# Later due times for the two halves of a unit's output projection, in an attention and gated-delta-rule kernel on one core

## The chip, the core and the metric

The kernel runs on one core of a Trainium2 chip. A core has five engines that run side by side, each with an instruction queue of its own: TensorE for matrix products (PE in the profile, its weight loads PEld), VectorE (DVE), ScalarE (ACT), GpSimd (POOL) and SyncE (SP), which here only starts DMA transfers. They meet through semaphores. An engine works through its queue in order: when the instruction at its head waits, all behind it wait too. Matrix products are written to PSUM, a small memory of eight banks; everything else lies in SBUF or in DRAM. The metric is the device time of one execution in microseconds, and lower is better.

## What is computed

A transformer block on 16 sequences of 128 tokens, 256 wide, all in fp32: attention, then a gated delta rule layer ("the unit work" below), then a feed-forward part with per-sequence adapters and rounded weights. The change lies in the second of these. Cut to what matters:

```
mixed = silu(causal_conv(hidden @ W_qkv));  q, k, v = split(mixed)   # 16 key heads, 32 value heads, 128 each
z     = hidden @ W_z
core  = chunk_gated_delta_rule(q, k, v, g, beta)                     # chunks of 64 tokens
core  = core * rsqrt(mean(core * core, -1) + 1e-6) * norm_w
x     = x + (core * silu(z)) @ W_out
```

The output projection of the title is the last product, with `W_out`. The sum of squares of `core` over its 128 channels is needed before it, for the root.

## The kernel before

**Units.** The delta rule is cut into 64 units: one key head (with its two value heads) for a group of four sequences, 512 tokens. Units run group by group, 16 key heads each. The projections of one group's 16 units add up in two PSUM banks, one for each pair of sequences; so each unit's output projection has two halves, `project(0)` and `project(1)` in `finish_unit`. A half is four products of 128x128 weights (`z`) with 256 columns (`wo_head`), which appear as eight instructions on the chip. After the sixteenth unit of a group DVE adds the bank to `x_in`, and SP stores it.

**Slots and due times.** The work of a unit is spread over eleven slots. In every slot a new unit is started, so that ten or so units are worked on at once, each at another step. A slot has 24 parts. The table `TIMES` gives, for each step of a unit, its due time in parts since the unit began; the due time modulo 24 is its place in the slot, and the quotient says how many slots later it comes. A heap (`events`, drained by `run`) calls the steps in order of due time, and so writes the program in that order. Steps for DVE that follow a product are put into the same heap by `later`, some parts after it.

The places in a slot that matter here, in order. Each step belongs to another unit:

| place | step | engine work, line |
|---|---|---|
| 5 | second gate `gate(1)` | product `ps_z` L812 |
| 8 | `new_values(0)`, `(1)` | products `ps_y` L823, ACT copies them to `y` L824 |
| 9 | first value projection `val(0)` | product L467, ACT's first convolution tap L476 |
| 9.5 | **`project(0)`** | products `ps_out` L873 |
| 11 | `attend(0)` | products `ps_ot` L829, ACT squares into `sq` L833 |
| 12 | `lower` | 32x32 products `ps_lo` L737, ACT copies `Mi` L740 |
| 13 | second value projection `val(1)` | L467, L476 |
| 14 | `attend(1)` | L829, L833 |
| 15.5 | **`project(1)`** | L873 |
| 16.5 | `norms` | products of ones with the squared q and k, `ps_n` L509 |
| 16.5 | `root` | products of ones with `sq`, `ps_r` L842: the sum of squares |
| 19 | `grow` | 32x32 products `ps_up` L749 to L751 |
| 19 | logarithms: a table load on ACT (L547), then exp and ln | L549 to L556 |
| 20, 22.5 | `products` of keys and queries | `ps_kq` L586 |

**From root to projection.** `root` leaves the sum of squares in PSUM. DVE adds a constant term into `r`, ACT turns it into a reciprocal root by ln and exp (L552, L553), SP writes it to DRAM in four small transfers (`scales`, L850) and reads it back spread over all partitions (`rb`, L852), and at place 4 of the next slot POOL multiplies the unit's `z` by it (`norm`, L864). Then its two projection halves may run.

**What sets the order.** The framework lays out each engine's queue when the program is built. It follows the order in which the program was written, but issues a later instruction first where by its own reckoning the earlier one isn't ready. DVE's queue is kept in written order by hand (`InOrder`), and on ACT the functions of the two activation tables are tied together (`follow`). PE's queue has no such ties. Of PSUM, six banks (`ps_b`) rotate over all products except the output projection's, whose two banks are apart (`ps_r`).

**Buffers.** `z` and `wo_head` have two buffers each, `rb` and `y` one. `wo_head` for a unit is loaded by SP (L437), which waits in its queue until the second half of the unit before last has read the old contents.

**One slot in four.** Four units share an inverse of 32x32 blocks (`inverse`), whose first rows are short DVE instructions that fall into one slot of each four.

Of the kernel before, what the change touches and what calls it, by code (L numbers as in the profile page):

```python
# [58 lines left out]
def tile_adaln_attn_ffn(  # L59
# [852 lines left out]
    def residual(g, t):  # L912
# [14 lines left out]
        "last": [194.0],  # L927
        "values": [177.0, 181.0, 183.5, 191.0, 194.5, 195.5],
        "outputs": [217, 221, 224, 224, 227, 230, 232.5, 236],
        "finish": [244, 249.5, 255.5],  # L930
        "logs": [19.0],
    }
    lag_of = lambda name, i: int(TIMES[name][i] // BEAT)
# [312 lines left out]
```

## Time and profile before

The time is 2249.76 us, the median of three executions (2246.99 to 2257.99). The profile is of one more execution, which took 2258.01 us; its span, from the first to the last instruction, is 2256.3 us.

| | us or share | where it is read |
|---|---|---|
| profiled execution, its span | 2258.01, 2256.3 | times; head of the page |
| mean granted PE clock | 0.980 | list of cores |
| projection `ps_out`, 1024 matmuls | 251.7 busy, 390 ns each | costliest groups |
| POOL `norm` of `z`, 64 instructions | 151.2 busy, 2362 ns each | costliest groups |
| ACT's reason for waiting longest on PE in the delta rule, `cv` L476 for `ps_in` L467 | 76.3 | costliest groups |
| DMA queue of SP | 28.0% of 16 engines | DMA queues |
| PE busy in 356 to 1665 us | 1280.03 of 1309.00 | stretches |
| PE busy in 1665 to 1882 us | 184.81 of 217.00 | stretches |
| PE busy in 1882 to 2256 us | 363.74 of 374.00 | stretches |

How such a profile is read: the page gives busy times and their groups; the list of waits says which engine stood still before which instruction and what ended that; and the timeline gives start and length in order. The ends of matmuls are modelled, so two that follow each other closely overlap by some 0.1 us in the list; starts are the firmer numbers. In a timeline the columns are start in us, length in us, engine, line, operation, what is written and read, shape of the weights and of the moving data, and the number of instructions merged; a bracket at the end gives the idle time before it and what ended it.

### The profile page before, as it was taken

What the parts mean: (1) busy time and instruction counts of PE and PEld (TensorE: products, weight loads), DVE (VectorE), ACT (ScalarE), POOL (GpSimd) and SP (SyncE); (2) the same over time, 40 slices, a digit from 0 to 9 for tenths busy, and PEclk for the clock granted to TensorE, in tenths of its full rate; (3) what the DMA queues carried; (4) which work ended last, traced back from release to release, by engine and by line L of the source; (5) the groups of instructions that cost most, each with busy time, mean ns of one, the idle gap of its engine ahead of it and who ended that gap; (6) DMA issues with size and microseconds to landing.
All of it is one profiled execution on the core that took longest, in us unless ns stands there. A gap on an engine that the chain in (4) does not pass through costs nothing. (4 is left out here: it accounts for less than half of the span.)

```text
span 2256.3 us, 41245 instructions
## 1 busy us (share of the span) xinstructions
PE 2127.2 (94%) x15992; PEld 1297.5 (58%) x15992; DVE 1404.9 (62%) x2194; ACT 1365.7 (61%) x2373; POOL 831.6 (37%) x573
## 2 busy tenths in 40 slices
PE   7898689999999999999999999999998987999999
PEld 3444356666666666666666666666665663344445
DVE  4788887677686867768686777868665321311111
ACT  4778577777777777777777777777775661111110
POOL 2233535445262544526254452625444115400000
PEclk9999889999999999999999999999999998999999
DMA  2210123333334434333433433334333314000000
GB/s 60 70 44 25 55 64 88 96 103 100 96 107 113 112 93 107 98 97 107 114 111 93 107 99 96 106 101 115 93 103 94 99 56 153 0 5 17 10 5 14
DMA packets 303250, 182.14 MB, mean 81 GB/s; under 512 B 189393, under 2 KB 283345, under 8 KB 303057
## 3 DMA queue, kind: packets, MB, share of 16 engines
q1 hardware_dynamic: 300848, 175.00, 28.0%
q0 software_dynamic: 1344, 4.20, 0.6%
q8 instruction: 128, 2.10, 0.4%
q14 instruction: 66, 0.53, 0.1%
q10 hardware_dynamic: 864, 0.31, 0.1%
HBM read 152.69 MB, written 5.77 MB: 70 GB/s over the span
## 5 line engine op out<-in xcount | busy, mean ns | idle before, releaser
L79 DVE SCALAR_TENSOR_TENSOR cv<-ps_in,cw,cv 128x508 f32<-128x508 f32 (+2 forms) x768 | 567.1, 740 | 297.4 <-ACT cv L476 279.3
L873 PE MATMUL ps_out<-wo_head,z 128*128 128x256 f32 x1024 | 251.7, 390 | 35.7 <-POOL z L864 35.5
L864 POOL TENSOR_TENSOR z<-z,rb 128x1024 f32<-128x1024 f32 x64 | 151.2, 2362 | 310.9 <-DMA rb<-scales 264.7
L467 PE MATMUL ps_in<-hT,w_qk 128*128 128x512 f32 x512 | 249.0, 610 | 5.3 <-DVE cv L79 2.4
L467 PE MATMUL ps_in<-hT,w_v 128*128 128x512 f32 x512 | 248.6, 607 | 0.0
L873 PEld LDWEIGHTS ps_out<-wo_head,z 128*128 128x128 f32 x1024 | 190.7, 194 | 99.6 <-POOL z L864 67.8
L812 PE MATMUL ps_z<-hT,w_gate 128*128 128x512 f32 x512 | 241.9, 594 | 0.3 <-ACT M L776 0.3
L476 ACT ACTIVATE cv<-ps_in,cw 128x512 f32<-128x512 f32 x256 | 174.9, 683 | 77.9 <-PE ps_in L467 76.3
L638 POOL TENSOR_TENSOR prod<-lanes,inv 128x512 f32<-128x512 f32 (+1 forms) x64 | 129.5, 2045 | 121.3 <-DVE inv L79 121.3
L525 POOL TENSOR_TENSOR o<-off,lk 128x16 f32<-128x16 f32 x64 | 13.9, 217 | 414.8 <-ACT lk L555 414.8
L812 PEld LDWEIGHTS ps_z<-hT,w_gate 128*128 128x128 f32 x512 | 95.8, 190 | 114.4 <-issue 101.1
L829 PEld LDWEIGHTS ps_ot<-aT,y 128*128 128x128 f32 x1024 | 134.5, 192 | 38.1 <-issue 28.5
L586 PE MATMUL ps_kq<-kq 128*128 128x256 f32 x512 | 134.8, 407 | 15.4 <-DVE cv L79 14.0
L467 PEld LDWEIGHTS ps_in<-hT,w_qk 128*128 128x128 f32 x512 | 94.1, 195 | 85.9 <-issue 66.5
L823 PEld LDWEIGHTS ps_y<-v,W 128*128 128x128 f32 x1024 | 124.5, 192 | 30.6 <-issue 22.9
L570 ACT ACTIVATE kq<-cv 128x512 f32<-128x512 f32 x128 | 80.7, 630 | 97.8 <-DVE cv L79 97.6
L829 PE MATMUL ps_ot<-aT,y 128*128 128x128 f32 x1024 | 135.6, 275 | 1.7 <-ACT y L824 1.7
L638 POOL TENSOR_TENSOR prod<-inv,gm 128x512 f32<-128x512 f32 (+1 forms) x64 | 127.9, 2023 | 15.3 <-DVE gm L79 15.3
L823 PE MATMUL ps_y<-v,W 128*128 128x128 f32 x1024 | 124.8, 275 | 0.0
L467 PEld LDWEIGHTS ps_in<-hT,w_v 128*128 128x128 f32 x512 | 87.5, 190 | 64.1 <-issue 61.2
L529 POOL TENSOR_TENSOR aT<-aT,o 128x1024 f32<-128x1024 f32 x64 | 121.8, 1902 | 5.1
L586 PEld LDWEIGHTS ps_kq<-kq 128*128 128x128 f32 x512 | 94.7, 197 | 34.5 <-issue 9.4
(202 smaller groups left out, 4069.0 us busy)
## 6 DMA issues: line engine op xcount, KB each, us to landing
aT<-sums SPq DMA_DIRECT2D x64, 512.0 KB
rb<-scales SPq DMA_DIRECT2D x64, 512.0 KB
w_qk<-in_w_qkv_dram SPq DMA_DIRECT2D x128, 128.0 KB
w_v<-in_w_qkv_dram SPq DMA_DIRECT2D x64, 256.0 KB
w_gate<-in_w_z_dram SPq DMA_DIRECT2D x64, 256.0 KB
wo_head<-in_w_out_dram SPq DMA_DIRECT2D x64, 256.0 KB
diag<-bT SPq DMA_DIRECT2D x256, 32.0 KB
W<-Uc SPq DMA_DIRECT2D x256, 32.0 KB
```

What stands on the lines that cost most here:

```text
L79: ins = getattr(self.engine, name)(*args, **kw)
L467: T.matmul(ps, lhsT=w[:, c, blk, :], rhs=hTs[g][:, c, :], start=c == 0, stop=c == ND - 1)
L476: A.activation(cv, psv, AF.Copy, scale=cw[:, col, 3:4])
L529: G.tensor_tensor(t4, t4, o.rearrange("p s h i -> p (s h) i")[:, :, :, None].to_broadcast([P, NP, 2, C]), ALU.subtract)
L570: ins = A.activation(dst, src, AF.Silu)
L586: T.matmul(ps[:, j, :, :], lhsT=d["kq"][:, s, 0, :], rhs=d["kq"][:, s, :, :], start=True, stop=True)
L638: G.tensor_tensor(out_tile, lhs[:, :, None, :].to_broadcast([P, r, c, j]), rhs.rearrange("p j c -> p c j")[:, None, :, :].to_broadcast([P, ...
L812: T.matmul(ps, lhsT=w_gate[u][:, c, h * P : (h + 1) * P], rhs=hTs[g][:, c, :], start=c == 0, stop=c == ND - 1)
L823: T.matmul(ps[:, j, :], lhsT=d["W"][:, p, :], rhs=v[:, p, :], start=True, stop=True)
L829: T.matmul(ps[:, s * S : (s + 1) * S], lhsT=d["y"][:, 2 * s + h, :], rhs=d["aT"][:, 2 * s + h, :], start=True, stop=True)
L864: G.tensor_tensor(d["z"], d["z"], d["rb"], ALU.mult)
L873: T.matmul(ps[:, j, :], lhsT=d["z"][:, h, s * S : (s + 1) * S], rhs=w_o[u][:, h, :], start=kh == j == h == 0, stop=kh == NK - 1 and j == h ...
```

## The change

Two due times are moved: the first half from 249.5 to 251.5, the second from 255.5 to 258.0. In places of a slot that is 9.5 to 11.5 and 15.5 to 18. POOL's `norm`, at 244, keeps its time. Nothing is computed differently, no buffer changes, and the slot in which each step falls stays the same (`lag_of("finish", ...)` and `LAST` are 10 before and after).

```diff
         "outputs": [217, 221, 224, 224, 227, 230, 232.5, 236],
-        "finish": [244, 249.5, 255.5],
+        "finish": [244, 251.5, 258.0],
```

In the order of due times, `project(0)` goes from behind `val(0)` to behind `attend(0)`, ahead of `lower`; `project(1)` goes from behind `attend(1)` to behind `norms` and `root`, ahead of `grow`. For the last unit of a group, the DVE addition into `x_in` and the store that follow a half move with it.

## The prediction

> **What bounds the kernel now.** I read the page's busy table first, then the costliest groups.
>
> ```profile
> PE 2127.2 (94%) x15992; PEld 1297.5 (58%) x15992; DVE 1404.9 (62%) x2194; ACT 1365.7 (61%) x2373; POOL 831.6 (37%) x573
> ...
> L873 PE MATMUL ps_out<-wo_head,z 128*128 128x256 f32 x1024 | 251.7, 390 | 35.7 <-POOL z L864 35.5
> ```
>
> TensorE (PE) is the bound, and the moved matmuls (L873, "the projection") are the group before which it idles longest. The busy time by stretch splits the run: 0 to 356 us attention and filling, 356 to 1665 the steady slots (PE busy 1280 of 1309 us), 1665 to 1882 draining, then the FFN. The change acts in the second and third. PE's waits inside the second:
>
> ```profile
> PE ps_kq L586 <- DVE cv L79: 14.0, 13, 1.6
> PE ps_out L873 <- POOL z L864: 11.2, 21, 1.1
> ```
>
> So two thirds of the 35.5 us lie outside the steady slots (10.6 of them before the last unit's projection alone). With PE 98% busy there, whatever PE gains or loses in a steady slot moves the end. One slot in PE's order of time (start, length, line):
>
> ```profile
> 997.73 1.99 PE L873 MATMUL ps_out<-wo_head,z 128*128 128x256 f32 x8
> 999.56 1.05 PE L829 MATMUL ps_ot<-aT,y 128*128 128x128 f32 x8
> 1000.54 0.69 PE L737 MATMUL ps_lo<-Tc,bT 32*32 32x32 f32 x32
> 1001.17 1.98 PE L467 MATMUL ps_in<-hT,w_v 128*128 128x512 f32 x4
> 1002.99 1.05 PE L829 MATMUL ps_ot<-aT,y 128*128 128x128 f32 x8
> 1003.88 1.89 PE L873 MATMUL ps_out<-wo_head,z 128*128 128x256 f32 x8
> 1005.70 0.64 PE L509 MATMUL ps_n<-sqa,ones 128*32 128x256 f32 x8
> 1006.16 0.61 PE L842 MATMUL ps_r<-sq,ones 128*32 128x256 f32 x8
> ```
>
> This is the source order of the due times: first half (9.5), attend 0 (11), lower (12), second value projection (13), attend 1 (14), second half (15.5), norms and root (16.5). The new times put the first half behind attend 0 and the second behind norms and root.
>
> **What the first half gains.** A unit's z is ready a nearly fixed time after its second value projection, and PE waits for it in the slots where DVE was late. Without a wait the half starts 0.43 us after the last value matmul. Over units 0 to 54 I summed what each start lies above that: 16.2 us. A half that waited also runs 1.99 instead of 1.89 us, 3.2 us in all. (The waits table says less because it counts from modelled ends, which overlap 0.16 us.) Behind attend 0 the half is due 0.89 us later (1003.88 less 1002.99); all but 1.0 us of the excess is smaller than that, and the later second part takes the rest. **Gain 19.4 us.** Attend 0 now needs y directly after the value projection. The copy of y ends 0.5 to 0.9 us early in half of the slots, 0.0 in a quarter, 0.2 us late in the last quarter; since the slot before it will be longer by what follows, I take 1 us of 0 to 3.
>
> **What the second half covered.** Root reads sq, which ACT squares from attend 1's bank. ACT in that slot:
>
> ```profile
> 1002.07 0.63 ACT L570 ACTIVATE cv<-cv 128x512 f32<-128x512 f32 x1
> 1002.72 1.28 ACT L547 ACT_TABLE_LOAD   x1
> 1004.01 0.69 ACT L476 ACTIVATE cv<-ps_in,cw 128x512 f32<-128x512 f32 x1
> 1004.60 0.59 ACT L833 ACTIVATE sq<-ps_ot 128x512 f32<-128x512 f32 x1
> ```
>
> Square waits behind the convolution's first tap and that behind a table load, and ends at 1005.19; root at 1006.16 is 0.97 us late for it only because the half lies between. With the half gone, norms follow attend 1 at once. Slot 9 has no projection yet (the first unit's comes in slot 10) and shows exactly this order:
>
> ```profile
> 333.58 1.05 PE L829 MATMUL ps_ot<-aT,y 128*128 128x128 f32 x8
> 334.57 0.64 PE L509 MATMUL ps_n<-sqa,ones 128*32 128x256 f32 x8
> 335.51 0.64 PE L842 MATMUL ps_r<-sq,ones 128*32 128x256 f32 x8 [0.31 <-ACT sq L833]
> ```
>
> There attend 1 to norms is 0.99 us, and root starts 0.05 us after square's end (335.46), leaving PE idle. In the steady slot: norms at 1002.99 + 0.99 = 1003.98, root could start 0.46 later (1006.16 less 1005.70), at 1004.44, and must wait until 1005.19 + 0.05 = 1005.24. **Stall 0.80 us.** Square ends 1.15 us after attend 1 in 41 of units 1 to 54. In the other 13, every fourth, the table load comes later, square ends at 1028.48 against an attend 1 begun at 1026.79, and the stall is 0.29 us; but there PE already idles 0.67 to 1.6 us a little later, before ps_kq, for a bank that DVE frees on its own time, so it is swallowed. Cost 41 x 0.80 = 32.8 us.
>
> Here two rules of the Trainium skill change the sum. "TensorEngine Tiling (Array Packing)", Key Properties, says tiles of one mode run in parallel but switching the mode drains TensorE. Parallel: the page's group rows give 398 ns for a norms matmul, and eight in series would cover 3.2 us and leave no stall; the timeline's 0.46 us shows the column strips beside each other. Drain: before, 128x128 goes to 128x32 to 32x32; now it goes to 128x32, back to 128x128 and to 32x32, one switch more per unit. The row for a switch is 0.99 less 0.89: 0.1 us, 93 ns in the finer steps, so 41 x 0.093 = 3.8 us (the 13 others again swallow it). "ScalarE: Activation LUTs", What ACT_TABLE_LOAD costs, puts a switch of tables at about 1.28 us plus a 1.38 us drain. By it square would end 1.38 us later, the stall would be 2.18 us and the sum 89 us (about 2323); in the trace the load takes 1.28 and the next activation starts 0.01 us after it, so 0.80 stands.
>
> **Does root's earlier place help z?** No: DVE makes r only after the second value convolution's taps (1004.73 to 1007.03), the norms' two operations and attend's product, at 1008.01; root had ended at 1006.77. **Queues passed.** SP holds wo_head's load until the second half has read the old weights: issued at 1005.80 before, about 1007.7 now; the next SP issue is at 1009.35, behind r, and an issue takes 0.37 us, so 1.3 us are spare. POOL's norm stays. The halves use two PSUM banks of their own, so the rotation of six keeps its order; norms and root wait only on ACT, whose copies of Mi end at 1002.05. DVE's eight sums into x_in come behind r instead of before it, at most a gain. Behind root on PE stand the second half, grow and ps_kq: all 0.9 us later, which is the cost above.
>
> **Drain.** There z is late by up to 3.8 us, and the half stands already where the compiler's planner thought z ready, so its due time matters little. Without norms, square is unfinished right after attend 1 and the second half goes first, as now. Where the planner let a projection break into a root, the rest of root now precedes the second half: I take -2 us of -5 to +2.
>
> Sum: 32.8 + 3.8 + 1 - 19.4 - 2 = +16.2 us on the profiled execution's 2258.0. That run lies 8.3 us above the median shown; added to the median 2249.8 it gives **2266.0 us**.
>
> **Rivals.** The order on an engine is the planner's: it keeps source order but takes a later instruction where it thinks the earlier not ready. On ACT the table load (due 19) runs ahead of a tap due 13 and a square due 14.
>
> *The half slips between norms and root* (14%), if the planner's own estimate has square unfinished after norms. Then root starts no earlier than now: no stall, but two extra switches, 41 x 0.2 = 8.2 us; 8.2 + 1.0 (excess left) + 3 (y) - 19.4 - 2 = -9.2: 2240.6, not slower. It decides from the point where norms are reckoned shorter than square's delay. For it: the real numbers, 0.46 against 1.15. Against it: slot 9, where grow was next and root still came first, with PE idling; and the drain:
>
> ```profile
> 1733.74 1.05 PE L829 MATMUL ps_ot<-aT,y 128*128 128x128 f32 x8
> 1737.16 0.91 PE L842 MATMUL ps_r<-sq,ones 128*32 128x256 f32 x2 [2.36 <-ACT sq L833]
> 1741.89 6.52 PE L873 MATMUL ps_out<-wo_head,z 128*128 128x256 f32 x16 [3.82 <-POOL z L864]
> 1748.34 0.63 PE L842 MATMUL ps_r<-sq,ones 128*32 128x256 f32 x6
> ```
>
> The projection entered after one quarter of a root, and again at 1844.38; two hits on a gap of 7 ns would be strange, so the planner seems to reckon the quarters in series, and norms as long enough.
>
> *Square moves up* (10%): attend 0 and its square come earlier, ACT is freer, and the table load falls behind the square, as it does in every fourth slot. Stall 0.29 us: 41 x 0.29 + 3.8 + 1 - 19.4 - 2 = -4.7, 2245. Against it: the load takes the hole while the second value projection still runs, and that hole stays.
>
> *The stall without the gain* (6%): z becomes later with PE (a later bank or load), and the wait stays: 32.8 + 3.8 = +36.6, 2286.
>
> **Numbers.** The stall has 70%; its own range is 2256 to 2280 (stall 0.6 to 1.0 us, gain 14 to 20). 0.5% is 11.2 us, about what a measurement tells from no change. Above 2261: 0.54 of the 0.70, and the last rival, 0.60. Below 2238.5: half of the first two rivals, 0.12. Between: 0.28. The range 2240 to 2284 leaves out half of the first rival, some of the last and the tails.
>
> **What would show it.** Right: root preceded by some 0.8 us idle for ACT sq in three of four slots, projection waits for POOL z nearly gone from the steady slots, ps_kq waits smaller, steady slots about 0.3 us longer on average. Wrong: the second half between norms and root, or square before the table load.

## The result, and the profile after

The changed kernel takes 2263.03 us (median of 15 executions, 2258.88 to 2268.5); the kernel before takes 2253.85 us in the same comparison (15 executions, 2246.99 to 2257.99). The ratio is 1.0044, interval 1.0035 to 1.0054: slower by 9.2 us where 16.2 were forecast. The profiled execution of the changed kernel took 2261.17 us, span 2259.5.

First the page's busy table and the row of the projection:

```profile
PE 2143.2 (95%) x15992; PEld 1281.6 (57%) x15992; DVE 1403.0 (62%) x2194; ACT 1362.1 (60%) x2373; POOL 832.6 (37%) x573
...
L873 PE MATMUL ps_out<-wo_head,z 128*128 128x256 f32 x1024 | 271.5, 399 | 28.7 <-POOL z L864 28.5
```

PE is busy 16 us longer with the same 15992 instructions, and the projection alone accounts for all of it: 271.5 us instead of 251.7, as the profile of before has it (the row stands in the prediction). So the products did not only wait elsewhere, they also ran longer. PE's list of waits in the steady slots (356 to 1665 us; us in total, times, longest):

```profile
PE ps_r L842 <- ACT sq L833: 4.2, 10, 0.6
PE ps_vt L795 <- DVE aT L79: 3.3, 3, 1.4
PE ps_kq L586 <- ACT W L753: 3.0, 3, 1.2
PE ps_kq L586 <- DVE cv L79: 2.2, 4, 1.4
PE ps_out L873 <- POOL z L864: 0.9, 3, 0.4
```

The projection's wait for z has gone (11.2 to 0.9 us), and the ps_kq wait for DVE has shrunk from 14.0 to 2.2 us (3.0 us before ps_kq now stand against ACT). But the stall that was to carry the loss, ps_r for ACT's sq, is 4.2 us in 10 slots and not 32.8 in 41. One slot in PE's timeline shows why:

```profile
1002.24 1.05 PE L829 MATMUL ps_ot<-aT,y 128*128 128x128 f32 x8
1003.23 0.64 PE L509 MATMUL ps_n<-sqa,ones 128*32 128x256 f32 x8
1003.80 0.70 PE L873 MATMUL ps_out<-wo_head,z 128*128 128x256 f32 x2
1004.50 0.64 PE L842 MATMUL ps_r<-sq,ones 128*32 128x256 f32 x8
1005.06 1.56 PE L873 MATMUL ps_out<-wo_head,z 128*128 128x256 f32 x6
```

The framework slipped one of the half's four products (two instructions) in between norms and root, and left three behind root. So it is in 50 of the 53 steady slots; in the other three (17, 33 and 49, the first slot of a group) two products slipped in. That is neither the order of the forecast (the whole half behind root) nor that of the first rival (the whole half between). It fills PE until the square is ready. ACT's timeline of the slot:

```profile
1001.97 1.28 ACT L547 ACT_TABLE_LOAD   x1
1003.27 0.69 ACT L476 ACTIVATE cv<-ps_in,cw 128x512 f32<-128x512 f32 x1
1003.85 0.59 ACT L833 ACTIVATE sq<-ps_ot 128x512 f32<-128x512 f32 x1
```

Square ends at 1004.44, as late behind attend 1 (2.20 us after its start) as before; root starts 0.06 us later, at 1004.50. ACT's order is as it was; what changed is PE's.

**Where the time went.** I cut each of the 53 steady slots (those of the projections of units 1 to 53, counted from one) at the starts of five PE groups and added up. Starts are used because the ends are modelled.

| stretch, us over 53 slots | before | after | difference |
|---|---|---|---|
| `val(0)` to `lower` (holds the first half) | 253.4 | 238.3 | -15.1 |
| `lower` to attend 1 | 129.5 | 129.5 | 0 |
| attend 1 to `grow` (holds the second half) | 196.9 | 232.0 | +35.1 |
| `grow` to `ps_kq` | 48.9 | 39.7 | -9.2 |
| `ps_kq` to the next `val(0)` | 679.8 | 674.1 | -5.7 |
| sum | 1308.5 | 1313.6 | +5.1 |

The two profiles differ by 3.2 us only, since the one of before has two stretches at lower clock that the other lacks: a mean granted clock of 0.83 in 330 to 350 us and 0.79 in 437 to 445, against 1.00 in the corresponding stretches of after. The profile of before starts its steady slots 3.4 us later, and its fourth slot takes 1.4 us longer (14.37 us from `ps_kq` where after has 12.95). If both are put down to the lower clock, the difference without them is 3.2 + 3.4 + 1.4 = 8.0 us, near the 9.2 of the medians.

### The profile page after: what moved, and what is told of

Read it like the earlier page. It is cut to its first block, busy times and chain, and to the rows that moved or that the text cites. A ratio compares the mean times of both kernels' runs of the same rounds, so it can differ in the third digit from the quotient of the medians.

```text
span 2259.5 us, 41250 instructions
## 1 busy us (share of the span) xinstructions
PE 2143.2 (95%) x15992; PEld 1281.6 (57%) x15992; DVE 1403.0 (62%) x2194; ACT 1362.1 (60%) x2373; POOL 832.6 (37%) x573
## 5 line engine op out<-in xcount | busy, mean ns | idle before, releaser
L873 PE MATMUL ps_out<-wo_head,z 128*128 128x256 f32 x1024 | 271.5, 399 | 28.7 <-POOL z L864 28.5
L467 PE MATMUL ps_in<-hT,w_v 128*128 128x512 f32 x512 | 248.2, 607 | 0.0
L873 PEld LDWEIGHTS ps_out<-wo_head,z 128*128 128x128 f32 x1024 | 182.9, 193 | 100.6 <-issue 48.6
L638 POOL TENSOR_TENSOR prod<-lanes,inv 128x512 f32<-128x512 f32 (+1 forms) x64 | 129.5, 2047 | 119.1 <-DVE inv L79 119.1
L1153 POOL TENSOR_TENSOR o<-o,x_in 128x512 f32<-128x512 f32 x8 | 10.1, 1265 | 279.3 <-DVE o L79 279.3
```

The lines of the kernel that those rows point to most:

```text
L467: T.matmul(ps, lhsT=w[:, c, blk, :], rhs=hTs[g][:, c, :], start=c == 0, stop=c == ND - 1)
L638: G.tensor_tensor(out_tile, lhs[:, :, None, :].to_broadcast([P, r, c, j]), rhs.rearrange("p j c -> p c j")[:, None, :, :].to_broadcast([P, ...
L873: T.matmul(ps[:, j, :], lhsT=d["z"][:, h, s * S : (s + 1) * S], rhs=w_o[u][:, h, :], start=kh == j == h == 0, stop=kh == NK - 1 and j == h ...
```

## The experiments

All runs compute the whole result. The kernel before took 2256.88 us beside e1 to e4 and 2256.42 beside the others. The stretches are summed as above; "rest" is `lower` to attend 1 and `ps_kq` to the next `val(0)`.

| kernel | us | ratio, interval | first half | second half | `grow` to `ps_kq` | rest | sum |
|---|---|---|---|---|---|---|---|
| before | | | 253.4 | 196.9 | 48.9 | 809.3 | 1308.5 |
| after | 2263.03 | 1.0044, 1.0035 to 1.0054 | 238.3 | 232.0 | 39.7 | 803.6 | 1313.6 |
| e1 | 2254.17 | 0.9993, 0.9980 to 1.0006 | 237.3 | 197.0 | 53.0 | 827.1 | 1314.5 |
| e2 | 2271.37 | 1.0064, 1.0042 to 1.0085 | 258.1 | 226.5 | 38.0 | 801.1 | 1323.8 |
| e3 | 2274.62 | 1.0088, 1.0066 to 1.0111 | 249.8 | 214.5 | 41.4 | 828.2 | 1333.9 |
| e4 | 2282.78 | 1.0119, 1.0098 to 1.0140 | 238.0 | 250.3 | 40.3 | 805.2 | 1333.9 |
| e5 | 2238.62 | 0.9918, 0.9903 to 0.9932 | 237.2 | 196.9 | 51.2 | 809.6 | 1294.9 |
| e6 | 2241.84 | 0.9925, 0.9910 to 0.9939 | 239.6 | 196.9 | 53.4 | 808.9 | 1298.7 |
| e7 | 2257.05 | 1.0002, 0.9991 to 1.0012 | 239.0 | 225.8 | 40.3 | 805.1 | 1310.1 |
| e9 | 2261.23 | 1.0015, 1.0004 to 1.0027 | 248.2 | 214.5 | 41.6 | 811.9 | 1316.2 |

And the second half's stretch in its three steps, mean us of the slots of the third place in each four (there the first half hardly waited, so little mixes in):

| kernel | attend 1 to norms | norms to root | root to `grow` | order |
|---|---|---|---|---|
| before | 2.71 | 0.46 | 0.54 | half, norms, root |
| after | 0.98 | 1.27 | 2.06 | norms, 1 product, root, 3 products |
| e2 | 0.98 | 1.63 | 1.63 | norms, 2 products, root, 2 products |
| e3, e9 | 0.98 | 2.49 | 0.57 | norms, half, root |
| e4 | 0.98 | 1.26 | 2.49 | norms, root, half |
| e7 | 0.98 | 0.76 | 2.49 | norms, root, half; square early |

**e1: the first half alone.** It asks whether the gain is there without the loss.

```diff
-        "finish": [244, 249.5, 255.5],
+        "finish": [244, 251.5, 255.5],
```

> Only the first half is moved (251.5), the second stays at 255.5. Both theories of the loss put it into the second half, so they agree here: attend 1 to grow stays 3.71 us in every slot, and the first half's lateness in the steady slots (18.6 us over 53 slots before) falls to about 2: 2253.9 - 16.5 = 2237 us. A rival says that the wait for z only hides DVE's lateness and is passed on to ps_kq or to y: then 2250 us and the waits before ps_kq (14.0 us) or ps_ot grow by what ps_out loses.

The steady gain came, 16.1 us in the first half's stretch, and yet the time didn't move. The three slots in which a group ends (16, 32, 48) grew from 78.5 us to 95.1 together, and that took back as much. One of them, DVE's timeline:

```profile
732.57 0.68 DVE L79 TENSOR_TENSOR x_in<-ps_out,x_in 128x512 f32<-128x512 f32 x1
...
739.78 0.69 DVE L79 TENSOR_TENSOR x_in<-ps_out,x_in 128x512 f32<-128x512 f32 x1 [3.66 <-DMA x_in<-in_x_dram]
...
741.74 0.25 DVE L79 TENSOR_SCALAR nn<-ps_n 128x128 f32<-128x128 f32 x1
```

SP's queue in the same stretch:

```profile
733.28 0.37 SPq L879 DMA_DIRECT2D x<-x_in  x1
733.74 0.42 SPq L437 DMA_DIRECT2D wo_head<-in_w_out_dram  x1
736.98 0.37 SPq L447 DMA_DIRECT2D x_in<-in_x_dram  x1
```

And PE, behind it:

```profile
736.50 2.98 PE L586 MATMUL ps_kq<-kq 128*128 128x256 f32 x8 [1.66 <-ACT W L753]
742.05 3.78 PE L467 MATMUL ps_in<-hT,w_qk 128*128 128x512 f32 x4 [2.57 <-DVE nn L79]
```

`x_in` has one buffer. After the first half DVE adds into it, SP stores it, and only then can SP load the other pair's `x_in`, which DVE needs after the second half. Sum to sum takes 7.2 us here; the halves now lie four parts of a slot apart instead of six, and DVE, in written order, stands 3.66 us with `nn` behind the wait. PE needs the bank that `nn` frees. Then the clock falls: `ps_in` takes 3.78 us where it takes 1.88 in an ordinary slot, and the mean granted clock in 735 to 750 us is 0.66.

**e2: the second half alone.**

```diff
-        "finish": [244, 249.5, 255.5],
+        "finish": [244, 249.5, 258.0],
```

> Only the second half is moved (258.0). The order laid out has two of its four products between norms and root in 41 slots. If the two moves add up (total +9.2, first half alone -16.5), this costs +25.7: 2279 us. If instead the slot's lengthening by 0.6 us alone already takes most of the wait for z away, whichever half causes it, the first half's gain is spent only once: +35 in attend 1 to grow, -9 before ps_kq, -14 of the wait for z: 2262 to 2266 us.

14.5 us slower, between the two forecasts. The waits for z stay, PE's list in the steady slots:

```profile
PE ps_out L873 <- POOL z L864: 14.3, 20, 1.9
```

So the second half's move does nothing for z and costs; the first half's move is what removes the wait. Root's stall is 1.0 us here, because in 40 of the 53 slots two products were slipped in before root instead of one. In the other 13, the fourth of each four, where square ends earlier, it was one.

**e3: the whole half between norms and root.** In these and the next runs two explanations of the 35 us stand against each other: that each stay of the half's 128x128 products inside the narrow run of norms, root and `grow` has a price of its own (about 0.3 us ahead of root and 0.2 behind it), or that only the prediction's 0.1 us for a switch and the stall count.

```diff
-        "keys": [0, 5.0, 9.5, 9.0, 15.0, 16.5, 32.5],
+        "keys": [0, 5.0, 9.5, 9.0, 15.0, 16.4, 32.5],
...
-        "finish": [244, 249.5, 255.5],
+        "finish": [244, 251.5, 256.45],
```

> The whole second half stands between norms and root (due 256.45, norms 16.4), the first at 251.5. Root comes when square has long ended, so there is no stall. Theory W (a stay of 128x128 products among the 128x32 ones costs 0.2 to 0.3 us beyond its own matmuls): attend 1 to grow 4.02 us in every slot, against 3.71, 2250 us. Theory S (the wait for square is the loss, a switch costs 0.09): 3.92 us in every slot, 2246 us.

From attend 1 to `grow` it takes 4.05 us in every slot, against 3.71 before: 0.34 more with no stall at all (root starts 0.73 us or more after square's end). The total was missed by 24 us. The halves are again too close at a group's end: its three slots take 93.8 us, 15.3 more than before, and the three behind them (17, 33, 49) 83.1 instead of 75.0. e9 repeats it without that.

**e4: the half held behind root.** A tie makes the forecast order come true:

```diff
-                T.matmul(ps[b], lhsT=ones, rhs=d["sq"][:, :, :, b], start=True, stop=True)
+                table["root"] = T.matmul(ps[b], lhsT=ones, rhs=d["sq"][:, :, :, b], start=True, stop=True)
...
+                    if n == 1 and j == h == 0:
+                        follow(ins, table["root"])
```

with the due times of the change.

> The first half at 251.5, the second at 258.0 and tied behind root's last product, so nothing can slip between norms and root: the order that the prediction had. Root then waits for square with PE idle, 0.80 us in three of four slots. As predicted (a switch 0.09): attend 1 to grow 4.60 us there, 2270 us. With theory W on top: 4.73 us, 2277 us. If the stall does not come, 3.9 us and 2246 us.

The predicted stall is there as soon as the predicted order is. PE's timeline of one slot, and the entry of its list of waits:

```profile
1013.96 0.64 PE L509 MATMUL ps_n<-sqa,ones 128*32 128x256 f32 x8
1015.22 0.64 PE L842 MATMUL ps_r<-sq,ones 128*32 128x256 f32 x8 [0.62 <-ACT sq L833]
1015.79 1.99 PE L873 MATMUL ps_out<-wo_head,z 128*128 128x256 f32 x8
```

```profile
PE ps_r L842 <- ACT sq L833: 29.8, 42, 1.2
```

Norms to root is 1.26 us instead of 0.46, so the stall is 0.80 us, as the prediction had it, and the list (which counts it from modelled ends) has it in 42 slots. In the first place of each four it is 1.11 us, in the fourth 0.40. The kernel is 25.9 us slower than before, more than the prediction's 16.2: from attend 1 to `grow` it takes 4.74, that is 3.71 + 0.80 + 0.23, not 3.71 + 0.80 + 0.09.

**e5 and e6: the first half alone, without the collision at a group's end.** e5 keeps the old times for the sixteenth key head; e6 moves all first halves and gives `x_in` two buffers, both loaded ahead.

```diff
-        "finish": [244, 249.5, 255.5],
+        "finish": [244, 251.5, 255.5],
...
-                plan(n - lag, make(at(lag)), TIMES[name])
+                edge_unit = name == "finish" and at(lag)[0] == NK - 1
+                plan(n - lag, make(at(lag)), [244, 249.5, 255.5] if edge_unit else TIMES[name])
```

```diff
-            if g == NG - 1:
-                load_x(g, 1)
+            load_x(g, 1)
...
-        kw = dict(tag="M2", bufs=2) if g == NG - 1 and n else dict(tag="x_in")
+        kw = dict(tag="M2", bufs=2) if g == NG - 1 and n else dict(tag=f"x_in{n}")
...
-                if n == 0 and g < NG - 1:
-                    load_x(g, 1)
```

> The first half at 251.5 for 60 units, and at its old 249.5 for the four that end a group. Theory X: the first half's gain is real, and moving it alone gave it back in the three slots where a group ends, because DVE's sum of the second half then waits for the second x_in, whose load can't start before the first half's sum is stored from the same buffer. Then the three slots fall from 95.1 us in all to the 78.5 of before, the rest keeps its gain of 10 to 14 us, and the time is about 13 us under the kernel before. If the gain was only passed on to DVE (the rival), it stays within 4 us of before.

> The first half at 251.5 for all units, but x_in has a buffer for each half and both are loaded before the group ends. Theory X: DVE does not wait for x_in, the three slots take 76 to 79 us, and the time is about 13 us under before, as with the four units left at their old time. If it is something else that moving the first half does at the end of a group (the bank, the store), the three slots stay near 95 us.

Both come out: 17.8 and 14.6 us faster than before, with 78.6 and 79.3 us for the three group ends. PE's list of waits in e5 no longer has z, and keeps the ps_kq wait, since nothing was added that could use it up:

```profile
PE ps_kq L586 <- DVE cv L79: 14.9, 17, 1.6
PE ps_in L467 <- DVE aT L79: 4.1, 16, 0.3
```

e5 and e6 can't be told apart (2236.53 to 2242.09 us, 2236.43 to 2243.34), and both beat the kernels before and after.

The two moves don't add up. e5's -17.8 and e2's +14.5 would make after 3 us faster than before, and it is 9 us slower. Of these 12.5 us, 5.5 lie in the second half's stretch (232.0 in after, 226.5 in e2, where two products instead of one fill the wait for the square). Where the rest lies was not shown.

**e7: as e4, with the table load held behind the square.**

```diff
         for ins in table["silus"]:
             follow(block[0], ins)
+        if "square" in table:
+            follow(block[0], table["square"])
...
-            A.activation(d["sq"][:, h].rearrange("p s t -> p (s t)"), ps, AF.Square)
+            table["square"] = A.activation(d["sq"][:, h].rearrange("p s t -> p (s t)"), ps, AF.Square)
```

> As the run with the second half forced behind root, and on ACT the table load is tied behind attend 1's square. If the table load is what makes square late, it ends 0.64 us after attend 1 in every slot instead of 1.15, the stall before root falls from 0.80 to 0.29 us, and attend 1 to grow takes 4.2 to 4.35 us in all slots instead of 4.74 (5.04): 41 x 0.5 = 20 us less than that run, 2262 us. If something else holds square, 4.74 us stays.

25.7 us faster than e4. ACT's timeline of one slot, and PE's:

```profile
1002.64 0.60 ACT L835 ACTIVATE sq<-ps_ot 128x512 f32<-128x512 f32 x1 [0.20 <-PE ps_ot L831]
1003.26 1.28 ACT L547 ACT_TABLE_LOAD   x1
```

```profile
1002.54 0.64 PE L509 MATMUL ps_n<-sqa,ones 128*32 128x256 f32 x8
1003.29 0.64 PE L844 MATMUL ps_r<-sq,ones 128*32 128x256 f32 x8
```

Norms to root is 0.76, a stall of 0.30 us where e4 has 0.80: the other half microsecond was the table load's place ahead of the square. It only brings the forecast order back to the level of before, though: its second half's stretch is still 28.9 us longer than before, by the stay of the half behind root and what is left of the stall, and the first half's gain (14.4) and the shorter waits behind `grow` (12.8) only just make up for it.

**e9: e6 with the whole half between norms and root**, the norms and second half at the due times of e3.

> The whole second half between norms and root again, now with two x_in buffers. Theories W and X together: attend 1 to grow stays 4.05 us, the slots at a group's end lose nothing, and the 20 to 25 us above the expectation of 2250 us vanish: 2248 to 2254 us, about the kernel before. If the half between norms and root costs more than its 0.34 us per slot in some other place, 2265 us or more stays.

The group ends are repaired (79.4 us instead of e3's 93.8), and attend 1 to `grow` is 4.05 again. The total is 7 us above the upper end of what was expected. Part of it can be placed, in PE's list of waits (lines are one lower here):

```profile
PE ps_out L872 <- POOL z L863: 7.9, 6, 1.9
```

The first unit's z in a group comes 20.1 to 22.1 us after the end of its root instead of 17.9, and ACT's ln and exp of `r` take 2 to 3.5 us together where they take 0.87 elsewhere: in slot 17 a convolution tap stands between them. Why ACT's order differs there stays open.

## Why the prediction was right or wrong

The direction and the range were right, in part by luck. Two terms of the sum were wrong and made up for each other in part: the stall was 26 us too high and the switch of mode 18 us too low. Of the prediction's own signs, the waits for z and ps_kq shrank as it said, but root's idle 0.8 us in three of four slots did not come, and the sign of being wrong, the second half between norms and root, came in part.

- **What the first half gains**: right in kind and nearly in size. 15.1 us in after, 16.1 and 16.2 in e1 and e5 where it stands alone, against 19.4 less 1 for y. The list has no wait of attend 0 for y in the steady slots. What is left of it lies in the first slot of each four (4.67 us from `val(0)` to `lower` against 4.43 in the others), where DVE is nearly full (below).
- **What the second half covered**: the stall of 0.80 us was the right price of the wrong order. e4 shows it to the hundredth when the half is held behind root. In after the framework issued one product between norms and root, and the stall fell to 0.06 us in two slots of four, about 0.35 in the first (14 slots), none in the fourth. Together that is 6.5 us (what the 35.1 leave beyond the 28.6 of the next point) instead of 32.8. The step that failed is the argument from slot 9 and the drain that the framework "seems to reckon ... norms as long enough" for the square: those places showed what it does when the next step is `grow` or when a root is already under way, not when four ready products stand behind root. e2, where fewer slip in when the square ends earlier, fits a reckoning that takes the square for unready after norms. But how it reckons readiness is not visible in a trace, and no run here settles it.
- **The switch of mode, 0.093 us per unit**: mis-sized. "TensorEngine Tiling (Array Packing)", Key Properties, in the Trainium skill says that a switch drains TensorE, and I priced it by the one switch that the trace of before shows. A stay of wide products inside the narrow run costs more. With 0.216 us for each of the half's instructions in a row (1.82 less 0.09 from half to norms in before, divided by eight), what is left over between norms and root is 1.21 - 0.46 - 2 x 0.216 = 0.32 us in after's slots without stall, 1.63 - 0.46 - 4 x 0.216 = 0.31 in e2, and 2.49 - 0.46 - 8 x 0.216 = 0.30 in e3. Between root and `grow` it is 2.06 - 0.54 - 6 x 0.216 = 0.22 in after, 0.23 in e2, 0.22 in e4. The price hangs on the place and not on the number of products. Two stays are 0.54 us per slot, 28.6 us in 53; the one switch ahead of norms only changes its place (0.98 less 0.89 before, now at attend 1). The weight loads (PEld) show where a part of the price arises. The first line is before, the second after:

```profile
1003.77 1.60 PEld L873 LDWEIGHTS ps_out<-wo_head,z 128*128 128x128 f32 x8
1003.79 0.30 PEld L873 LDWEIGHTS ps_out<-wo_head,z 128*128 128x128 f32 x2 [0.41 <-issue]
```

  In all 53 slots of before the half's first load starts 0.11 us ahead of its first product (1003.88), under attend 1's products, and root's first load 0.21 us ahead of root, under the norms. In after both start with their product (1003.80 for the half), so neither load is hidden. 0.11 + 0.21 is as much as a stay ahead of root costs. For the stay behind root this explains 0.11 of the 0.22; the rest is open, and no run tests it.
- **Swallowed by the ps_kq wait**: right, and more than reckoned. The fourth slots lose 0.55 us at the second half and get 0.71 back before ps_kq.
- **In some slots another engine is nearly full**: missed. The mean slot by its place in the four (without slots 4, 16, 32 and 48, which the lower clock and the group ends lengthen):

| place | before | after | e5 |
|---|---|---|---|
| first | 24.96 | 24.93 | 24.62 |
| second | 24.30 | 24.42 | 23.81 |
| third | 23.87 | 24.41 | 23.82 |
| fourth | 25.17 | 24.88 | 25.13 |

  In the first place after's stretches trade against each other: unit 17 has 5.07 us in the first half's and 4.24 in the second half's stretch, unit 53 has 4.43 and 4.86, and both slots last 24.95 to 24.98. The second half's stretch is 0.89 us longer there on average, but 0.34 comes back behind ps_kq (12.93 to 12.59) and 0.57 in the first half's stretch. So nearly the full 0.60 us is paid in the third place alone; in the second, the first half's 0.48 covers most of it. The prediction's 41 x 0.893 assumed it in three places of four. In slot 25 of after, a first one, DVE is busy 23.41 of 24.93 us and PE 24.40; in the two slots behind it DVE is busy 14.50 and 13.40 us and PE all of 24.4. So DVE probably holds the first place. It is not shown: with e4's longer stall the first place grew to 25.35 us, so PE counts there too.
- **Queues passed**: the statement that DVE's later sums into `x_in` are "at most a gain" holds for after only because both halves moved (sums some 6.5 parts apart; DVE waits 2.5 us for x_in in two groups). e1 shows the same step as a loss of 16.6 us. On SP one item was missed: at a group's end the second half's store now goes ahead of the root's four transfers.

```profile
739.29 0.37 SPq L879 DMA_DIRECT2D x<-x_in  x1
739.75 2.68 SPq L850 DMA_DIRECT2D scales<-r  x4
```

  `r` was ready at 738.07, so `scales` waits 1.7 us, and z comes 19.84 us after root's end instead of 17.91. It falls into slots of the first place (17, 33, 49), which last 24.65 to 24.98 us like their like, so no cost is seen.
- **Drain**: -2 was taken, and the part behind the last steady slot is 1.4 us longer in after (594.8 against 593.4 us), 1.3 longer in e2 and 4.9 shorter in e5 (588.5). By these single profiles, with stretches at lower clock in the drain (a mean of 0.95 over 1665 to 1882 us in after), the first half's move helps there and the second half's does not; the prediction treated them together.
- **Rivals**: "the half slips between norms and root" was half true, one product of four. Its price of two switches at 0.2 us together should be 0.34 by e3, and for after's split 0.54. At e3's price over 53 slots (18.0 us instead of 8.2) its -9.2 becomes +0.6, and e9, which has that order without the group-end loss, is at 1.0015. "Square moves up" is what e7 builds: its stall of 0.29 us was right (0.30), its total of 2245 was not (2257.05), mostly for the same missing price of the stay.

Sum over the steady slots: first half -15.1, stays +28.6, stalls +6.5, given back in the last two stretches of the table -14.9 (of it 1.4 the lower clock in the profile of before), in all +5.1.

Set beside the forecast: 16.2, less 26.3 for the stall, plus 17.8 for the stays (21.6 us in the 40 slots outside the fourth place, instead of 3.8), plus 3.3 for the smaller gain of the first half, plus 3.4 for the drain, less 6.5 given back beyond the fourth place's stays and the clock's 1.4. That is 7.9 us, where the profiles differ by 8.0 without the lower clock.

## What to carry to other kernels

Move only the step that waits. The first half had a wait of z to lose and gained 0.8% alone (e5); the second had none, and its new place cost 14.5 us alone (e2) and 27 on top of e5's gain. Before moving a product group in among products of another tile shape, price the stay from entry to exit, not one switch, and ask what the framework will do with the group when the step in front of it isn't ready. And follow a moved step to its rarest use: three group ends out of 53 slots decided whether e1 was 0% or 0.8% faster.

## What the runs showed of the hardware

- A stay of 128x128 products among 128x32 products cost 0.30 to 0.32 us between norms and root, and 0.22 to 0.23 between root and the 32x32 products, whether two, four, six or eight instructions stayed. The single switch from 128x128 to 128x32 costs 0.09.
- PE's clock fell on short gaps, but not on each. In before PE stood still for 1.60 us ahead of `ps_kq` (438.29 to 439.90 us) and the granted clock was 0.79 in 437 to 445; in e5 it stood still for 1.60 us at the same step, and the clock was 1.00 in the same stretch. In e1 gaps of 1.66 and 2.57 us at a group's end went with a granted clock of 0.66 over 735 to 750 us. "TensorE: Matmul & The Clock Gate" in the Trainium skill (Part 1: The HAM clock gate) puts the fall behind an idle window of about 3.4 us. None of these gaps was that long, and the two of 1.60 us ended differently, so the length of one gap doesn't decide it here.
- A lost microsecond on DVE at a group's end cost PE more than itself: the three group-end slots of e1 lost 16.6 us behind 10.6 us of DVE waiting for `x_in`. The granted clock was 0.66, 0.66 and 0.89 over the 15 us there (from 735, 1131 and 1528 us); how much of the loss is the clock's was not separated.
- Between products of one shape the next weights are loaded ahead: the half's first load leads its product by 0.11 us behind attend 1 (before), and by nothing behind the 128x32 products (after).
